# The extra block of a quantile graph network: 16-bit words from the collection, one tree for three quantiles, half candidates in three tiles

## The chip, the cores and the metric

The kernel runs on one core of one Trainium2 chip. The metric is device time in microseconds (us). PE is TensorE (matmuls; PEld its weight loads), DVE VectorE, ACT ScalarE, POOL GpSimd, SP SyncE, which here issues DMAs. SBUF is the on-chip memory that the engines work in, PSUM the banks that TensorE writes to.

## The reference, cut to what matters

There are 16 graphs ("batches") of N = 1024 nodes with C = 64 channels and a dense 0/1 adjacency. Four layers follow each other, each of the form x = x + layer(relu(layernorm(x))). Layer 0 thins out the neighbours of a node, sorts the values of those that remain in each channel, and takes three quantiles, each between two order statistics:

```python
vals = jnp.where(nd[..., None], x[:, None, :, :], jnp.inf)
s = jnp.sort(vals, axis=2)
nv = nd.sum(2)
for tau, w in zip((0.25, 0.5, 0.75), (0.25, 0.5, 0.25)):
    pos = tau * jnp.maximum(nv - 1, 0)
    lo, hi = floor(pos), ceil(pos)
    v_lo, v_hi = s[..., lo, :], s[..., hi, :]        # cut: take_along_axis
    agg = agg + w * (v_lo + (pos - lo) * (v_hi - v_lo))
out = x + agg
y = relu(out @ W1 + b1) @ W2 + b2
```

So six order statistics (three quantiles, lower and upper) are wanted for each of 16 x 1024 x 64 places. Layers 1 to 3 are a gated unit, a small network over summed neighbours, and an attention, all with dense products with the adjacency.

## The kernel before, in words

**How an order statistic is found.** The nodes of a batch are sorted once per channel (`sort_pair`, L760-855). The sorted list of a channel is cut into words of neighbouring ranks, 56 in all (NW; 28, NH, in each half). For a node, one fp8 matmul over the neighbours (`ndT` from `prepare`, L858-957) and the words' weights (`wt`, `weights`, L958-) gives for each word and channel a number that holds both a count and a part of the place (L1096). ACT adds the wanted rank (the bias) and writes 16-bit integers (L1104). Among these DVE looks for the last word that is not past the rank: it adds 2048 for the second statistic of the quantile (L1162), and takes a tree of unsigned maxima over the words (L1167). Small integer arithmetic on the result (`places`, L1010-) gives masks. PE transposes the 16-bit words, ACT takes their sign (L1149, L1151), and matmuls with a table of the sorted values (L1196) leave for each channel a row of candidates in PSUM, from which DVE picks one with masked copies (`pick`, L1060-1068; L1204 in select) and adds it with its factor to `agg` (`add_to`, L1069-1073).

**A window and the extra block.** In `select` each quantile looks only at a window of the words. A few nodes need more; they are flagged, and up to 64 of them in a batch (ROOM) are done once more over all 56 words. `compact` (up to L1302) runs at the end of each batch's `select`: it numbers the flagged nodes, writes the flags (L1237), gathers their neighbour rows, forms the words with the same weights (L1287, seven pieces of 512 numbers), copies each piece from PSUM to `xr` as 32-bit numbers (L1291), and SP stores one or two pieces to the DRAM buffer `x_d` (L1292). It also stores a selection matrix, transposed, to `sel_d`. The first batch of a pair has partitions 0 to 63, the second 64 to 127, so a pair's extra rows are one tile. `x_d` has one place, used again in each pair.

`extras` (L1304-1371), the block that is changed, then does both batches' extra rows at once:
- four DMAs on ACT's queue (L1307) load `x_d` into `comb_x`, 128 x 3584 32-bit numbers; DVE clears two tables (L1311), and SP loads the values into them, four DMAs each; `qx` (L1319) is the bias for three quantiles
- for each quantile k: ACT writes `y_x` (L1325), 16 transposes (L1332) go to a `tr` tile, two signs (L1335) are taken, DVE adds 2048 (L1339), takes a tree of maxima over 28 rows (L1003 and L1007 in `maxima`), and the last two operations give `z_x` and `odd_x` (L1345, L1346)
- `places` for all six statistics together
- for each of six statistics: 64 matmuls fill `cand` (L1356; one tile of four PSUM banks), five masked copies pick (L1064), one operation adds to `agg_x` (L1071, L1073)
- for each of the two batches: SP loads `sel_t` (L1364, one buffer), eight matmuls in fp32 put the rows back at their nodes (L1367; 16 records on PE), and a masked copy writes them into `aggs[i]` (L1368).

**The order of work.** A loop over 8 pairs (L1619-1654) calls `weights` and `select` for both batches, `extras`, and `layers` for both (L1466-1585; the first operation that needs `aggs` is L1471), and in the same scope `prepare` and `sort_pair` for the next pair. A scheduler lays out a fixed order on each engine at build time, by priorities and estimated times, so work of the next pairs is interleaved with `extras` and `layers`. Each engine runs its list in order; SP's and ACT's lists also hold the DMAs that they issue, and a DMA issue that waits holds up what is behind it. Tiles are reused as soon as their last reader is done, which the waits express. The neighbour tables of the layers are loaded by SP (L1452); the weights start with a load of `y_d` (L965), which the end of `sort_pair` (L847, L852, L853, L855) stores, an addition (L969) and the weights themselves (L974).

A general branch behind the loop does a batch again where there were more than 64 flagged nodes; it isn't entered with this input.

Of the kernel before, what the change touches and what calls it, by code (L numbers as in the profile page):

```python
# [9 lines left out]
F32 = mybir.dt.float32  # L10
BF16 = mybir.dt.bfloat16
# [12 lines left out]
P = 128  # L24
# [10 lines left out]
NW = 56  # L35
# [7 lines left out]
def gnn_stack(ctx, tc, x, adj, nodemask, w, out):  # L43
# [24 lines left out]
    nc.vector.tensor_scalar(offdiag, ident, -1.0, 1.0, op0=ALU.mult, op1=ALU.add)  # L68
    ones_b = const.tile([P, N], BF16, name="ones_b")
    nc.vector.memset(ones_b, 1.0)  # L70
# [90 lines left out]
    nc.vector.memset(ttab, 0.0)  # L161
    x_d = dram.tile([P, NW * C], F32, name="x_d")
    sel_d = dram.tile([2, P, NT, P], F32, name="sel_d")
# [291 lines left out]
    def general(gw):  # L455
# [47 lines left out]
        with tc.For_i(0, B, 1) as b:  # L503
            with ExitStack() as per_batch:
# [13 lines left out]
                with (  # L518
# [4 lines left out]
                    kept = nb1.tile([P, NT, N], BF16, name="kept")  # L523
                    notrem = nb1.tile([P, NT, N], BF16, name="notrem")
                    for t in range(NT):
                        a = nb2.tile([P, N], F32, name="a", bufs=3)
# [9 lines left out]
                        cum = nb2.tile([P, N], F32, name="cum")  # L536
                        nc.vector.tensor_tensor_scan(cum, ones_b, ni, 0.0, op0=ALU.mult, op1=ALU.add)

# [520 lines left out]
    def pick(cand, masks):  # L1059

        v = cand.rearrange("p q (d l) -> p q d l", l=24)
        for (dst, frm, n), mk in zip(PICKS, masks):
            mk = mk.rearrange("p (q d o) -> p q d o", d=4, o=1)
            nc.vector.copy_predicated(  # L1064
                v[:, :, :, dst : dst + n], mk.to_broadcast([P, NQ, 4, n]), v[:, :, :, frm : frm + n]
            )
        return v[:, :, :, 11]
# [158 lines left out]
    def compact(b, i, wt, row10, out_of, kept, cp, cpp):  # L1226
# [39 lines left out]
        nc.vector.tensor_copy(who, pv[:, 9:10])  # L1266
        nc.scalar.copy(vx[mine, :], pv[mine, :9])
        rows = cp.tile([P, N], F8, name="rows")
        nc.gpsimd.indirect_dma_start(
# [3 lines left out]
        for j0 in range(0, NT, 4):  # L1273
# [5 lines left out]
            nc.scalar.copy(ndx[:, j0 : j0 + 4, :], px, saturate=False)  # L1279
        for u in range(0, len(PIECES), 2):  # L1280
            two = PIECES[u : u + 2]
            n = len(two) * 512
            xr = cp.tile([P, 1024], F32, name="xr")
            for e, g in enumerate(two):
                pw = bank()
                for j in range(NT):
                    nc.tensor.matmul(  # L1287
                        pw, ndx[:, j, :], wt[g][:, j].rearrange("p w c -> p (w c)"),
                        start=(j == 0), stop=(j == NT - 1),
                    )  # L1290
                nc.scalar.copy(xr[mine, e * 512 : (e + 1) * 512], pw[mine])  # L1291
            nc.sync.dma_start(x_d[mine, two[0] * 512 : two[0] * 512 + n], xr[mine, :n])  # L1292
        sel_t = cp.tile([P, NT, P], F32, name="sel")
# [7 lines left out]
    def extras(pr, kept, aggs, xs, xp):  # L1301

        vx = kept["vx"]
        comb = xs.tile([P, NW * C], F32, name="comb_x")  # L1304
        for u in range(0, len(PIECES), 2):
            at = slice(PIECES[u] * 512, (PIECES[u] + len(PIECES[u : u + 2])) * 512)
            nc.scalar.dma_start(comb[:, at], x_d[:, at])  # L1307
        tabs = []
        for i in range(2):
            tab = xs.tile([4 * NH, NQ, 4, 48], F16, name=f"tab{i}")  # L1310
            nc.vector.memset(tab, 0.0)  # L1311
            for d in range(4):
                taken = nc.sync.dma_start(
                    tab[d : 4 * NH : 4, :, d, :],
                    t_d[(pr * 2 + i) * C : (pr * 2 + i + 1) * C, :NH].rearrange("(q d) h e -> d h q e", d=4)[d],
                )
            tabs.append(tab)
        qx = xs.tile([P, 3], F32, name="qx")
        nc.vector.tensor_scalar(qx, vx[:, :3], -2048.0, -2048.0, op0=ALU.mult, op1=ALU.add)  # L1319
        signs = []  # L1320
        z = xs.tile([P, 1, 6, C], U16, name="z_x")
        odd = xs.tile([P, 1, 6, C], U16, name="odd_x")
        for k in range(3):
            y = xs.tile([P, 2, 2 * NQ, 4 * NH], I16, name="y_x", bufs=2)
            nc.scalar.activation(  # L1325
                y[:, 0].rearrange("p r (h d) -> p r h d", d=4),
                comb.rearrange("p (h r d) -> p r h d", r=2 * NQ, d=4),
                AF.Identity, bias=qx[:, k : k + 1], scale=1.0,
            )
            pt = xp.tile([P, 2, 512], F32, name="tr").bitcast(BF16).rearrange("p e (q n) -> p (e q) n", n=P)  # L1330
            for q in range(NQ):
                nc.tensor.transpose(pt[: 4 * NH, q, :], y[:, 0, q, :].bitcast(BF16), ident_b)  # L1332
            for s in range(2):
# [4 lines left out]
                signs.append(sign)  # L1338
            nc.vector.tensor_scalar_add(y[:, 1], y[:, 0], 2048.0)  # L1339
            yu = y.bitcast(U16)  # L1340
            maxima(yu, NH)
            ev, od = yu[:, :, :NQ, :4], yu[:, :, NQ:, :4]
            zs = z[:, 0, 2 * k : 2 * k + 2, :].rearrange("p s (q d) -> p s q d", d=4)
            os_ = odd[:, 0, 2 * k : 2 * k + 2, :].rearrange("p s (q d) -> p s q d", d=4)
            nc.vector.tensor_tensor(zs, ev, od, op=ALU.max)  # L1345
            nc.vector.tensor_tensor(os_, od, ev, op=ALU.is_gt)  # L1346
        marks = places(xs, z, 6 * C, 1)
        aggx = xs.tile([P, C], F32, name="agg_x")
        ag = aggx.rearrange("p (q d) -> p q d", d=4)
        for s in range(6):  # L1350
            cand = xp.tile([P, NQ, P], F32, name="cand")
            for q in range(NQ):
                for part in range(2):
                    for i in range(2):
                        mine = slice(i * ROOM, (i + 1) * ROOM)
                        nc.tensor.matmul(  # L1356
                            cand[mine, q, :96], signs[s][:, q, mine], tabs[i][:, q, :, part * 24 : (part + 1) * 24],
                            start=(part == 0), stop=(part == 1),
                        )
            v = pick(cand[:, :, :96], [mk[:, 0, s, :] for mk in (odd, *marks)])  # L1360
            add_to(ag, s == 0, v, vx[:, 3 + s : 4 + s])
        for i in range(2):
            sel_t = xs.tile([P, NT, P], F32, name="sel_t")
            nc.sync.dma_start(sel_t, sel_d[i])  # L1364
            ps = xp.tile([P, 2, 512], F32, name="tr")[:, 0, :].rearrange("p (t c) -> p t c", c=C)
            for t in range(NT):
                nc.tensor.matmul(ps[:, t, :], sel_t[:, t, :], aggx, start=True, stop=True)  # L1367
            nc.vector.copy_predicated(  # L1368
                aggs[i], kept["flag"][i].rearrange("p (t o) -> p t o", o=1).to_broadcast([P, NT, C]), ps
            )  # L1370
# [331 lines left out]
```

## Time and profile before

| | |
|---|---|
| median of three runs | 5883.57 us (5877.19 to 5884.53) |
| the profiled execution | 5867.21 us |
| its span, first to last instruction | 5865.4 us |
| mean granted TensorE clock | 0.84 of full speed |
| ACT busy | 3801.4 us (65%) |
| PE busy | 4372.7 us (75%) |
| L1325, ACT, 128x3584 | 24 times, 3277 ns |
| L1291, ACT, 64x512 | 112 times, 580 ns; idle before them 134.6 us for the stores x_d |
| L1356, PE, 112x96 | 3072 matmuls, 109.3 us |
| L1064, DVE, 128x768 / 128x256 / 128x128 / 128x64 | 956 / 420 / 287 / 221 ns |
| L1367, PE, one batch | 3.65 us |

The page gives busy time of an engine as a share of the span, and digits for 40 slices, where 9 means 90% or more. A stretch's line gives the busy time of each engine in it. A line of the timeline gives the start, the length, engine, line of code, operation, output and inputs, shapes and number of instructions; in brackets stands how long the engine was idle before and what released it. Events that the text uses, in us from the start of the span:

| pair (0 to 7) | its first L1096 | second flags L1237 | first memset L1311 | end of the second L1368 |
|---|---|---|---|---|
| 3 | 2373.0 | 2748.7 | 2802.3 | 2909.8 |
| 4 | 3072.8 | 3448.1 | 3498.9 | 3609.1 |
| 5 | 3779.4 | 4154.7 | 4207.4 | 4316.3 |
| 7 (last) | 5193.8 | 5548.2 | 5591.1 | 5668.7 |

### The profile page before, as it was taken

How to read it: one execution, taken by the hardware profiler on the slowest of the kernel's cores; microseconds unless marked ns; L12 is line 12 of the kernel's file. 1: busy time of each engine (PE TensorE's matmuls, PEld its weight loads, DVE VectorE, ACT ScalarE, POOL GpSimd, SP SyncE). 2: the span in 40 equal slices, each digit the busy share in tenths (PEclk: the TensorE clock that was granted, in tenths of full speed). 3: DMA queues.
4: the chain of work that ended last, by engine and by line, in shares of the span. 5: the costliest groups of instructions: out<-in, count | busy, mean ns of one | idle time of the engine just before them, and what ended most of it. 6: DMA issues, size and time to landing. Idle time of an engine off the chain costs nothing.

```text
span 5865.4 us, 114417 instructions
## 1 busy us (share of the span) xinstructions
PE 4372.7 (75%) x45010; PEld 2736.6 (47%) x45010; DVE 5066.1 (86%) x13175; ACT 3801.4 (65%) x5752; POOL 180.9 (3%) x292
## 2 busy tenths in 40 slices
PE   1488677885868857788577876788677895878856
PEld 1355443554435544455434554355443554435532
DVE  9899888988899897998889988899888998877744
ACT  1587657676576855777567666677657775577724
POOL 3000000000000000000000000000000000000000
PEclk5699778997889968899689986899878997789967
DMA  4401273013631056210561125501264013620023
GB/s 127 125 27 41 89 221 116 27 31 124 207 98 36 20 156 217 63 40 29 172 203 45 37 77 168 172 35 34 89 206 132 27 32 120 208 81 19 11 88 127
DMA packets 524420, 568.23 MB, mean 97 GB/s; under 512 B 263808, under 2 KB 413568, under 8 KB 523872
## 3 DMA queue, kind: packets, MB, share of 16 engines
q1 hardware_dynamic: 381472, 476.43, 26.0%
q10 hardware_dynamic: 140064, 81.84, 4.6%
q8 instruction: 355, 5.82, 0.4%
q0 software_dynamic: 2336, 2.57, 0.2%
q14 instruction: 193, 1.58, 0.1%
HBM read 376.95 MB, written 183.76 MB: 96 GB/s over the span
## 4 chain that ended last, share of the span: by engine, by line
PE 27%; DVE 23%; ACT 14%; DMA 10%; issue 3%; SPq 0%; POOL 0%; ACTq 0%; DVEq 0%; POOLq 0%
PE comb L1096 7%; DVE y L1167 5%; PE cand L1196 4%; DMA adjT<-a_d 4%; PE bank L1459 4%; ACT sign L1151 3%; PE comb L1287 3%; DMA a_d<-at 2%; ACT y L1104 2%; DVE cand L1204 2%; DVE att L1570 2%; DVE adjT L1563 1%; DVE y L1162 1%; DVE cum L878 1%; DVE wt L974 1%
## 5 line engine op out<-in xcount | busy, mean ns | idle before, releaser
L1096 PE MATMUL comb<-wt,ndT 128*128 128x512 fp8e5 x6144 | 1422.3, 383 | 119.5 <-ACT sign L1151 98.1
L1104 ACT ACTIVATE y<-comb,qb 128x512 int16<-128x512 f32 x1152 | 742.5, 711 | 479.4 <-PE comb L1096 479.0
L1096 PEld LDWEIGHTS <-ndT 128*128 128x128 fp8e5 x6144 | 587.6, 98 | 837.4 <-issue 196.9
L1196 PE MATMUL cand<-vtab,sign 128*128 128x48 f16 (+1 forms) x18432 | 678.8, 192 | 60.9 <-DVE agg L1071 32.4
L1196 PEld LDWEIGHTS <-sign 128*128 128x128 fp8e5 x18432 | 651.5, 97 | 118.6 <-issue 57.2
L1151 ACT ACTIVATE sign<-comb,lower 128x1024 fp8e5<-128x1024 int16 (+1 forms) x640 | 693.2, 1083 | 0.0
L1151 ACT ACTIVATE sign<-comb,half 128x1024 fp8e5<-128x1024 int16 (+1 forms) x640 | 688.0, 1075 | 0.0
L1167 DVE TENSOR_TENSOR y<-y 128x512 uint16<-128x512 uint16 (+5 forms) x896 | 668.7, 788 | 16.6 <-PE comb L1149 16.2
L1204 DVE COPY_PREDICATED cand<-w_f,cand 128x256 f32<-128x256 uint16 (+1 forms) x1536 | 533.7, 376 | 95.8 <-PE cand L1196 92.6
L886 ACT COPY at<-pk 128x512 f32<-128x512 f32 x256 | 147.4, 586 | 394.5 <-PE pk L884 219.0
L1149 PE MATMUL comb<-ident_b,y 128*128 128x128 bf16 x4608 | 318.1, 222 | 93.5 <-ACT sign L1151 59.6
L1459 PE MATMUL bank<-adjT,nd 128*64 128x512 f32 x1024 | 314.1, 668 | 77.6 <-DMA adjT<-a_d 75.7
L1149 PEld LDWEIGHTS <-y 128*128 128x128 bf16 x4608 | 294.6, 99 | 118.9 <-issue 117.9
L928 PE MATMUL pk<-minus_b,rem 128*128 128x128 bf16 x1024 | 225.3, 246 | 158.2 <-ACT rem L909 158.2
L1459 PE MATMUL bank<-att,hs 128*64 128x512 f32 x512 | 199.9, 863 | 155.0 <-ACT hs L1575 154.9
L928 PE MATMUL pk<-ident_b,ni 128*128 128x128 bf16 x1024 | 220.5, 243 | 122.0 <-ACT ndT L934 65.0
L878 DVE TENSOR_TENSOR_SCAN cum<-ni 128x1024 f16<-128x1024 fp8e5 x128 | 291.8, 2283 | 11.0 <-POOL ni L874 10.9
L884 PE MATMUL pk<-ident,a 128*128 128x128 f32 x1024 | 189.5, 336 | 136.8 <-DMA a<-in_adj_dram 102.5
L974 DVE TENSOR_SCALAR wt<-node 128x2048 uint8<-128x2048 f16 x224 | 268.8, 1216 | 13.9 <-PE comb L1287 13.7
L774 DVE TENSOR_TENSOR s<-s 128x512 f32<-128x512 f32 (+1 forms) x440 | 275.6, 626 | 0.0
L1162 DVE TENSOR_SCALAR y<-y 128x4608 int16<-128x4608 int16 x128 | 173.4, 1355 | 118.0 <-ACT y L1104 117.7
L775 DVE TENSOR_TENSOR s<-s 128x512 f32<-128x512 f32 (+1 forms) x440 | 274.4, 624 | 0.0
(373 smaller groups left out, 8301.5 us busy)
## 6 DMA issues: line engine op xcount, KB each, us to landing
adjT<-a_d SPq DMA_DIRECT2D x384, 512.0 KB
a<-in_adj_dram SPq DMA_DIRECT2D x128, 512.0 KB
a_d<-at ACTq DMA_DIRECT2D x256, 256.0 KB
m_d<-swapped SPq DMA_DIRECT2D x104, 512.0 KB
swapped<-m_d SPq DMA_DIRECT2D x104, 512.0 KB
n_d<-nat SPq DMA_DIRECT2D x128, 128.0 KB
x_d<-xr SPq DMA_DIRECT2D x48, 256.0 KB
comb_x<-x_d ACTq DMA_DIRECT2D x24, 512.0 KB
```

Of the source, the lines that this page charges most:

```text
L774: nc.vector.tensor_tensor(to_lo, lo, hi, op=ALU.max)
L878: nc.vector.tensor_tensor_scan(cum[:, t - t0, :], ni[:, t, :], wide[:, t, pad - 1 : pad - 1 + N], 0.0, op0=ALU.add, op1=ALU.add)
L928: nc.tensor.matmul(pk[:, n % 4, :], lhs, rhs, start=(n % 4 == 0 and m == 0), stop=(m == len(terms) - 1 and last),)
L974: nc.vector.tensor_scalar(wt[g][:, :, k : k + 4, :].bitcast(U8), node, 4.0 * (25 + CODE * (8 * g + k)), 4.0 * 26, op0=ALU.add, op1=ALU.min,)
L1096: nc.tensor.matmul(pw, ndT[:, j, t * P : (t + 1) * P], wt[1 + g8][:, j].rearrange("p w c -> p (w c)"), start=(j == 0), stop=(j == NT - 1),)
L1104: nc.scalar.activation(y[:, 0, chunks, at : at + 8 * d_].rearrange("p q (w d) -> p q w d", d=d_), pw.rearrange("p (w q d) -> p q w d", w=8 ...
L1149: nc.tensor.transpose(pt[:, q - q0, :], y[:, 0, q, :].bitcast(BF16), ident_b)
L1151: nc.scalar.activation(signs[tl][s][:, q0:q1, :], pt.bitcast(I16), AF.Sign, bias=before[s], scale=-1.0, saturate=False,)
L1167: nc.vector.tensor_tensor(v[:, :, :, :n], v[:, :, :, :n], v[:, :, :, n : 2 * n], op=ALU.max)
L1196: nc.tensor.matmul(cand[:, e, at : at + 12 * d_].rearrange("p (d l) -> p d l", l=12), signs[tl][sec][:, chunk, :], tab[:, q, :, half_ * 12 ...
L1204: nc.vector.copy_predicated(v[:, :, :, dst : dst + k], mk.to_broadcast([P, 2, C // 2, k]), v[:, :, :, frm : frm + k])
L1459: nc.tensor.matmul(po[to : to + C, :], lhs, rhs[:, f * HALF : (f + 1) * HALF], start=(j == 0), stop=(j == NT - 1))
```

## The change

- `compact` writes 16-bit integers at once: for each piece three ACT operations, one for each quantile, with the bias `qx` (now made there by DVE), in an order of elements in which a chunk's 32 words lie together. `xr` has two buffers, and each piece is stored by itself (7 stores a batch, 14 a pair; now 8).
- `x_d` holds [128, 7 pieces, 3 quantiles, 512] 16-bit numbers. `extras` loads them with 12 DMAs on ACT's queue straight into `y_x`, for all three quantiles. L1325 and `comb_x` are gone.
- POOL clears the tables instead of DVE.
- The 48 transposes read strided words out of `y_x`; all of them, and the candidates and the last products, use three tiles of two PSUM banks (`two`).
- One addition of 2048 for all three quantiles, one tree for all six statistics; z and odd come from four operations.
- Candidates are made and picked in halves of 8 chunks, so 12 halves with 32 matmuls, five masked copies and one accumulation each.
- Both `sel_t` are loaded by two DMAs on ACT's queue into the place of `y_x`, ahead of the candidates.
- A constant row of ones is shortened from 1024 to 128 columns; the general branch makes its own.

```diff
-    x_d = dram.tile([P, NW * C], F32, name="x_d")
+    x_d = dram.tile([P, 7, 3, 512], I16, name="x_d")
...
         nc.scalar.copy(vx[mine, :], pv[mine, :9])
+        qx = cp.tile([P, 3], F32, name="qx")
+        nc.vector.tensor_scalar(qx[mine], pv[mine, :3], -2048.0, -2048.0, op0=ALU.mult, op1=ALU.add)
...
-            xr = cp.tile([P, 1024], F32, name="xr")
...
-                nc.scalar.copy(xr[mine, e * 512 : (e + 1) * 512], pw[mine])
-            nc.sync.dma_start(x_d[mine, two[0] * 512 : two[0] * 512 + n], xr[mine, :n])
+        for g in PIECES:
+            xr = cp.tile([P, 3, 512], I16, name="xr", bufs=2)
...
+            for k in range(3):
+                nc.scalar.activation(
+                    xr[mine, k].rearrange("p (h d r) -> p h r d", h=4, d=4),
+                    pw[mine].rearrange("p (h r d) -> p h r d", r=2 * NQ, d=4),
+                    AF.Identity, bias=qx[mine, k : k + 1], scale=1.0,
+                )
+            nc.sync.dma_start(x_d[mine, g], xr[mine])
...
-        comb = xs.tile([P, NW * C], F32, name="comb_x")
-        for u in range(0, len(PIECES), 2):
-            at = slice(PIECES[u] * 512, (PIECES[u] + len(PIECES[u : u + 2])) * 512)
-            nc.scalar.dma_start(comb[:, at], x_d[:, at])
+        y = xs.tile([P, 2, 3, 7, 512], I16, name="y_x")
+        for g in (1, 3, 5, 0):
+            for k in range(3):
+                here = slice(g, g + (2 if g else 1))
+                nc.scalar.dma_start(y[:, 0, k, here], x_d[:, here, k])
...
-            nc.vector.memset(tab, 0.0)
+            nc.gpsimd.memset(tab, 0.0)
...
-            y = xs.tile([P, 2, 2 * NQ, 4 * NH], I16, name="y_x", bufs=2)
-            nc.scalar.activation(
-                y[:, 0].rearrange("p r (h d) -> p r h d", d=4),
-                comb.rearrange("p (h r d) -> p r h d", r=2 * NQ, d=4),
-                AF.Identity, bias=qx[:, k : k + 1], scale=1.0,
-            )
-            pt = xp.tile([P, 2, 512], F32, name="tr").bitcast(BF16).rearrange("p e (q n) -> p (e q) n", n=P)
+            pt = xp.tile([P, 1024], F32, name="two", bufs=3).bitcast(BF16).rearrange("p (q n) -> p q n", n=P)
+            by_word = y[:, 0, k].rearrange("p g (w r) -> p r (g w)", w=16)
             for q in range(NQ):
-                nc.tensor.transpose(pt[: 4 * NH, q, :], y[:, 0, q, :].bitcast(BF16), ident_b)
+                nc.tensor.transpose(pt[: 4 * NH, q, :], by_word[:, q].bitcast(BF16), ident_b)
...
-            nc.vector.tensor_scalar_add(y[:, 1], y[:, 0], 2048.0)
-            yu = y.bitcast(U16)
-            maxima(yu, NH)
+        nc.vector.tensor_scalar_add(y[:, 1], y[:, 0], 2048.0)
+        yu = y.bitcast(U16).rearrange("p s k g n -> p (s k) g n")
+        for n, m in ((3, 4), (2, 2), (1, 1)):
+            nc.vector.tensor_tensor(yu[:, :, :n], yu[:, :, :n], yu[:, :, m : m + n], op=ALU.max)
+        yw = yu[:, :, 0]
+        for n in (256, 128):
+            nc.vector.tensor_tensor(yw[..., :n], yw[..., :n], yw[..., n : 2 * n], op=ALU.max)
...
         marks = places(xs, z, 6 * C, 1)
+        sel_t = xs.tile([P, 2, 3, 7, 512], I16, name="y_x").rearrange("p s k g n -> p (s k g n)")
+        sel_t = sel_t[:, : 4 * NT * P].bitcast(F32).rearrange("p (i t n) -> p i t n", i=2, n=P)
+        for i in range(2):
+            nc.scalar.dma_start(sel_t[:, i], sel_d[i])
         aggx = xs.tile([P, C], F32, name="agg_x")
...
-            cand = xp.tile([P, NQ, P], F32, name="cand")
-            for q in range(NQ):
+            for q0 in range(0, NQ, 8):
+                cand = xp.tile([P, 1024], F32, name="two", bufs=3).rearrange("p (q n) -> p q n", n=P)
+                for q in range(8):
...
-            v = pick(cand[:, :, :96], [mk[:, 0, s, :] for mk in (odd, *marks)])
-            add_to(ag, s == 0, v, vx[:, 3 + s : 4 + s])
+                here = slice(q0 * 4, (q0 + 8) * 4)
+                v = pick(cand[:, :, :96], [mk[:, 0, s, here] for mk in (odd, *marks)])
+                add_to(aggx[:, here].rearrange("p (q d) -> p q d", d=4), s == 0, v, vx[:, 3 + s : 4 + s])
         for i in range(2):
-            sel_t = xs.tile([P, NT, P], F32, name="sel_t")
-            nc.sync.dma_start(sel_t, sel_d[i])
-            ps = xp.tile([P, 2, 512], F32, name="tr")[:, 0, :].rearrange("p (t c) -> p t c", c=C)
+            ps = xp.tile([P, 1024], F32, name="two", bufs=3)[:, : NT * C].rearrange("p (t c) -> p t c", c=C)
             for t in range(NT):
-                nc.tensor.matmul(ps[:, t, :], sel_t[:, t, :], aggx, start=True, stop=True)
+                nc.tensor.matmul(ps[:, t, :], sel_t[:, i, t, :], aggx, start=True, stop=True)
```

## The prediction

> **What bounds the kernel now.** I read the page first (engine shares, the 40 slices), then a table of 20 us stretches over one middle pair of batches, then the groups by shape, and last the timeline of the last pair around the extra block.
>
> ```profile
> span 5865.4 us, 114417 instructions
> ...
> PE 4372.7 (75%) x45010; PEld 2736.6 (47%) x45010; DVE 5066.1 (86%) x13175; ACT 3801.4 (65%) x5752; POOL 180.9 (3%) x292
> DVE  9899888988899897998889988899888998877744
> ```
>
> DVE carries 86% of the span; only the last three slices fall off: those are the layers of the last pair, where nothing is left to lie beside them. So there are two regimes. In pairs 0 to 6 a pair takes about 705 us (first L1096 of pair 4 at 3072.8 us, of pair 5 at 3779.4), of which DVE idles some 77. There the price of an edit is mostly its DVE work, and what it moves counts only if DVE stalls. After the last pair's extra block comes a chain of latencies up to the end of the program. Stretches from pair 3's extra block into pair 4's select (columns: length, busy PE, PEld, DVE, ACT, POOL, clock, DMA share, GB/s):
>
> ```profile
> 2800.00:2820.00 20.00, 2.29 (x18) 1.87 (x17) 14.87 (x30) 8.54 (x5) 1.76 (x4) 0.56 0.60 179
> 2840.00:2860.00 20.00, 11.79 (x133) 9.35 (x133) 19.83 (x54) 14.12 (x27) 0.53 (x1) 0.66 0.34 111
> 3020.00:3040.00 20.00, 15.19 (x155) 8.02 (x154) 12.87 (x42) 15.06 (x20) 0.00 (x0) 1.00 0.79 253
> 3220.00:3240.00 20.00, 16.54 (x176) 10.03 (x172) 20.00 (x55) 19.27 (x31) 0.00 (x0) 1.00 0.10 36
> ```
>
> The extra block lies in the first two. DVE loses 5 us in the first and nothing in the second, since sorting and neighbour work of later pairs is interleaved there. DVE loses more at 3020 to 3040 (the end of the layers and the way into the next weights) than in the extra block. In select it is full. The last pair has nothing to interleave (start, us, engine, line, form, idle before and its releaser):
>
> ```profile
> 5594.13 6.46 ACT L1325 ACTIVATE y_x<-comb_x,qx 128x3584 int16<-128x3584 f32 x2 [12.74 <-DVE qx L1319]
> ...
> 5628.29 2.77 PE L1356 MATMUL cand<-tab,sign_x 112*64 112x96 f16 x64 [13.82 <-DVE agg_x L1071]
> 5631.10 0.96 DVE L1064 COPY_PREDICATED cand<-odd_x,cand 128x768 f32<-128x768 uint16 x1 [2.87 <-PE cand L1356]
> ...
> 5664.30 3.65 PE L1367 MATMUL tr<-agg_x,sel_t 128*128 128x64 f32 x16 [3.83 <-DMA sel_t<-sel_d]
> 5667.99 0.72 DVE L1368 COPY_PREDICATED agg<-flag,tr 128x512 f32<-128x512 uint16 x1 [6.76 <-PE tr L1367]
> 5668.61 0.68 DVE L1471 TENSOR_TENSOR nd<-nd,agg 128x512 f32<-128x512 f32 x1
> ```
>
> The reader sees PE and DVE taking turns over one `cand` tile (2.87 us waiting in each turn, five turns), and the second `sel_t` load waiting for its buffer. All of it is ahead of the first layers' operation, with no cover.
>
> **Last pair, step by step.** DVE leaves select at 5590.9 in both versions.
> (1) The collection. Now each piece needs an ACT copy of 0.58 us (L1291, 64x512) and waits for its store (3.05 us at 5576.8, with one buffer). Afterwards there are three 16-bit copies a piece: nearest row L1291's 0.58, above it the permuted L1104 with 0.71. That is 28 copies more a pair, 16 to 24 us of ACT, against waits for stores of 134.6/8 = 16.8 us a pair that the second buffer takes away, and 3 x 3.28 = 9.8 us of L1325 that goes. I take ACT as even. The gather grows from 4 issues to 12, and from 1.83 to 2.75 MB; 4 issues now take 3.28 us in pair 3, so 8 more cost up to 6.6, most of them before the last store. The data landed at 5588.8; I take 5591, with 5588.8 and 5595.4 as ends.
> (2) L1325 in front of DVE and PE goes: DVE now begins L1339 at 5597.44, afterwards at about 5591.
> (3) Add and tree: rows 3584 in 1.09 us; maxima of 3584 in 2.02 and 1792 in 1.085, so 0.15 us plus 0.52 ns an element. Now 3 x (1.09 + 4.5) = 16.8 us. Afterwards one add (2.9 to 3.3) and maxima of 9216, 6144, 3072, 1536, 768: 11.6. With four z/odd operations (1 us) z is ready at about 5607; now 5619.6.
> (4) `places` with the first picks took 5619.7 to 5627.7, so 8 us: 5615. Signs do not come later: 48 transposes (16 in 1.96 us) end at 5597, six signs of 1.96 end at about 5605. They read strided words, which no row shows; were transposes twice as slow, signs would end near 5607, still ahead. POOL's clearing of `tab` (nearest: its 128x2048 memset, 1.80 us) should be done by 5596 (an estimate from that row, twice, with 1.5 for the larger tile), and the tables landed before the first mask.
> (5) Candidates: half a tile is 32 matmuls of 43 ns, 1.39 us on PE. Three tiles let PE run ahead by three halves. A half's picks cost 0.152 us plus elements/0.96 GHz for 384, 128, 128, 64 and 32, and an accumulate: 1.77 us when each waits for the former. The new DVE order weaves two halves; where select does that now, two picks take 2.98 us. I take 1.45 for PE and DVE together. Some two of twelve halves lie in `places`, ten follow: last accumulate at 5629.5 (now 5656.7).
> (6) Both `sel_t` loads go ahead on ACT's queue into the place of y_x. Two groups of 3.65 follow directly, then L1368: layers begin at about 5638, now 5668.6.
> The sum is **30 us less**. With the late landing and 1.8 us a half: 22; with picks at 1.2 and the early landing: 35. Layers behind it wait for this operation, and SP, no longer holding a `sel_t` load back, issues their first loads sooner; I see no cause for them to give it back, but their table loads (L1452) could land no earlier: then up to 8 us return.
>
> **Pairs 0 to 6.** DVE work per pair: two memsets of 1.338 go (-2.7), add -0.3, tree -1.9, picks +2.3 (36 operations more, 0.065 us each as woven) to +6.7 (at 1.77). Net -2.6 to +1.8, so about zero.
> What matters is the order (numbers of pair 3 into pair 4). I charged the DVE order of both built programs, from the end of select, with rows' durations. From the second flags (L1237) to the add it is 49.6 now, 50.7 then. From there to the last L1368 it shrinks from 86.7 to 50.2 us: the cover (24 us of sorting, 10 of neighbours) moves behind the block. The block would then end some 36 us sooner, at 2874 instead of 2909.8. It must now run on its own pace, about the 47 us of the last pair; DVE work of 50 still covers it.
> The layers are a chain of 201 us (2909.8 to about 3111). Started 36 us earlier, it ends near 3075. But the first weights operation L974 now has 40 us of layers work before it and 35 behind; then all 75 lie before it. DVE work up to L974 grows from 259 to 293 us: at 2748.7 + 293 and the stalls of now (48 us less the 6 to 8 that the block gives up) 3083 to 3089, now 3056. From L974 to the next flags it falls from 368 to 333; with the 24 us of stalls that lie there now, the next flags come at 3440 to 3446, now 3448.
> One new stall: the last sorting operation leads over L847, L852, L853 (1.05 + 0.66 + 0.59 at least) to the store L855, the load `node` L965 and then L969. Now 23.6 us of DVE work cover this, then 4.7. In pair 3 it takes from L811 at 3022.7 to past 3041, with PE full; if alone, from these durations and two transfers, 9 to 11. So 4 to 6 us of stall, 14 at worst (flags then at 3444 to 3460), and PE, whose weights come later, idles some 13 us that select does not ask for while DVE is full.
> The bounds per pair: -8 (the stalls in the block go, nothing new) to +10 (the chain exposed, the picks at 1.77). I take **-2** (3446), between the sums without and with the new stall, so -14 over seven pairs.
>
> **Rules against it.** The rows say 0.152 us fixed for a pick and 0.065 where woven. The Trainium skill, "VectorE: DVE Perf Modes", section "The TRN2 errata", says that each instruction pays its latency again and that small tiles should be avoided; from its measured 150 cycles I estimate 36 x 0.156 = 5.6 us a pair, 3 more than by the woven row, in all 26 us less gain. The clearing of `tab` leaves DVE for POOL (1.80 us nearby). "SBUF — State Buffer", section "SBUF: two separate sides", says that a GpSimd instruction and a DVE instruction in a two-port mode block each other entirely; by it some of the 2.7 us would come back as waiting. No row of before has the two side by side.
>
> **Rivals.**
> (a) Forecast: tail -30, pairs -2 each: 5867.2 - 30 - 14 = 5823. Chance 0.48.
> (b) The block's stalls in the middle pairs are won too (11 us of idle DVE there now), -8 each with the same tail: 5867.2 - 30 - 56 = 5781. For: the turns of 2.87 us vanish there as well. Against: the second stretch above has DVE at 19.83 of 20. Chance 0.20.
> (c) Nothing: the woven picks or the ACT copies (28 x 0.71 = 20 us, in select where ACT has 19.27 of 20) cost 4 a pair: 5867.2 - 30 + 28 = 5865. Chance 0.15.
> (d) Slower: the chain from sorting to L969 stands open in each pair, and the layers' own gaps, no longer beside weights, add to it: 10 a pair, 5867.2 - 30 + 70 = 5907. It decides from 30/7 = 4.3 us a pair. For: DVE at 12.87 of 20 in that place already; against: PE and ACT work of the next pair starts early enough to feed select. Chance 0.17.
>
> **Numbers.** The profiled execution took 5867.2 us (span 5865.4); the median of the three runs is 5883.6, 16.4 more, which I add: (a) 5840, (b) 5798, (c) 5881, (d) 5924. The likeliest, 5840, has its own range of 5812 to 5868 (per pair -6 to +2). The range for 8 in 10 takes in (b) with some of its spread and (c), and half of (d): 5786 to 5912. Within 0.2% (11.8 us, about what a measurement can tell) is (c); faster (a) and (b), 0.68; slower (d), 0.17.
>
> **What would show it.** In the last pair: first layers' operation (L1471 of before) at about 5638; z by 5607; candidate halves 1.4 to 1.5 apart; no wait for `sel_t`. In middle pairs: last L1368 about 36 us earlier, L974 about 30 later, next flags within 8 of now, and a DVE wait for `node` of 4 to 6 us. I am wrong if y lands after 5596, if halves come 1.8 or more apart, or if that wait is over 10 us.

## The result, and the profile after

The changed kernel is slower: 6329.03 us in the median of four runs (6307.92 to 6335.03) against 5883.25 us, a ratio of 1.0753 (95% interval 1.0727 to 1.0780). The forecast was 5840 us, a gain. The profiled execution took 6327.28 us.

The page of the changed kernel, the lines that answer to those of before (the last two give the busy share of DVE and ACT in 40 slices):

```profile
span 6325.4 us, 115008 instructions
...
PE 4544.1 (72%) x45010; PEld 2805.8 (44%) x45010; DVE 5087.1 (80%) x13319; ACT 4410.8 (70%) x5952; POOL 236.7 (4%) x308
...
DVE  9997689886897968977789777897778976886744
ACT  2578757786678756787577784678757787578844
```

DVE does the same work (5087 us, 5066 before) in a span that is 460 us longer, so it waits. ACT does 609 us more. The groups by shape say which: first the changed kernel's copies out of PSUM, the transposes that wait for them, and the masked copies of select (columns: busy us, mean ns of one, idle before and its releaser),

```profile
L1293 ACT ACTIVATE xr<-comb,qx 64x512 int16<-64x512 f32 x336 | 757.8, 2694 | 46.1 <-PE comb L1288 45.9
...
L1206 DVE COPY_PREDICATED cand<-w_f,cand 128x256 f32<-128x256 uint16 x1024 | 416.9, 424 | 527.6 <-PE cand L1198 525.7
...
L1303 PE MATMUL comb<-ident,sel 128*128 128x128 f32 x128 | 35.7, 434 | 139.8 <-ACT xr L1293 139.8
```

then the copies and the masked copies of before:

```profile
L1204 DVE COPY_PREDICATED cand<-w_f,cand 128x256 f32<-128x256 uint16 x1024 | 418.4, 421 | 94.8 <-PE cand L1196 92.6
...
L1291 ACT COPY xr<-comb 64x512 f32<-64x512 f32 x112 | 61.8, 580 | 201.5 <-DMA x_d<-xr 134.6 <-PE comb L1287 66.9
```

One copy takes 2694 ns, not 580 to 711. The records of neighbours overlap a little, so the 336 of them keep ACT busy for 757.8 us (2.26 each), where 112 took 61.8. How that reaches DVE is seen in stretches over a `compact` and the extra block of pair 3 of the changed kernel (columns as above: length, PE, PEld, DVE, ACT, POOL, clock, DMA share, GB/s):

```profile
2980.00:3000.00 20.00, 8.06 (x23) 3.19 (x22) 0.71 (x2) 20.00 (x10) 0.00 (x0) 0.75 0.18 44
3000.00:3020.00 20.00, 10.10 (x158) 9.57 (x158) 11.49 (x27) 19.45 (x12) 1.39 (x2) 0.67 0.29 89
3060.00:3080.00 20.00, 6.03 (x63) 4.47 (x63) 20.00 (x54) 15.00 (x27) 0.00 (x0) 0.50 0.24 79
3315.00:3335.00 20.00, 8.99 (x116) 6.01 (x112) 11.69 (x60) 7.23 (x12) 0.00 (x0) 0.67 0.36 73
```

In the first, ACT is busy all 20 us with ten instructions and DVE does 0.71 us. In the third, the extra block itself, DVE is full: the block is not where the time goes. The fourth is the way into the next weights, where DVE idles 8 of the 20 us. The timeline of the last pair's `compact` shows the links of the chain:

```profile
6018.27 40.37 ACT L1293 ACTIVATE xr<-comb,qx 64x512 int16<-64x512 f32 x18 [2.85 <-PE comb L1288]
...
6038.66 3.35 PE L1288 MATMUL comb<-wt,ndx 128*128 128x512 fp8e5 x8 [3.39 <-ACT xr L1293]
6045.32 1.12 PE L1303 MATMUL comb<-ident,sel 128*128 128x128 f32 x4 [3.31 <-ACT xr L1293]
...
6051.98 1.12 PE L1303 MATMUL comb<-ident,sel 128*128 128x128 f32 x4 [5.42 <-ACT xr L1293]
6052.89 3.40 PE L1198 MATMUL cand<-vtab,sign 128*128 128x48 f16 x69
6055.52 1.55 DVE L1206 COPY_PREDICATED cand<-w_f,cand 128x256 f32<-128x256 uint16 x4 [27.96 <-PE cand L1198]
```

18 copies stand on ACT for 40 us. PE's next piece needs a PSUM tile that ACT has not emptied, the transposes of the selection matrix (L1303) too, and in PE's fixed order the last candidates of select (L1198) are behind those. DVE waits 27.96 us for them. Over the whole execution DVE waits 525.7 us for L1198, where it waited 92.6 us for the same matmuls (L1196) before.

From the second flags of pair 0 to those of pair 7 a pair takes 762.7 us, 702.5 before: 60.2 more, seven times, is 421 of the 460 us. Pair 0 up to its second flags gives 30, the stretch from the last pair's flags to the end 8.

### The profile page after: what moved, and what is told of

It reads as the page before. It is cut to its first block, busy times and chain, and to the rows that moved or that the text cites. A ratio compares the mean times of both kernels' runs of the same rounds, so it can differ in the third digit from the quotient of the medians.

```text
span 6325.4 us, 115008 instructions
## 1 busy us (share of the span) xinstructions
PE 4544.1 (72%) x45010; PEld 2805.8 (44%) x45010; DVE 5087.1 (80%) x13319; ACT 4410.8 (70%) x5952; POOL 236.7 (4%) x308
## 3 DMA queue, kind: packets, MB, share of 16 engines
q0 software_dynamic: 2336, 2.57, 0.2%
## 4 chain that ended last, share of the span: by engine, by line
PE 32%; DVE 27%; ACT 24%; DMA 11%; issue 5%; POOL 0%; SPq 0%; ACTq 0%; DVEq 0%; POOLq 0%
PE comb L1098 12%; ACT xr L1293 9%; ACT sign L1153 6%; DMA adjT<-a_d 5%; PE cand L1198 5%; DVE y L1169 4%; PE bank L1469 4%; ACT y L1106 2%; DVE cand L1206 2%; DMA a<-in_adj_dram 2%; PE pk L930 2%; DVE wt L976 1%; DVE cum L880 1%; DVE att L1580 1%; DVE y_x L1340 1%
## 5 line engine op out<-in xcount | busy, mean ns | idle before, releaser
L1098 PE MATMUL comb<-wt,ndT 128*128 128x512 fp8e5 x6144 | 1483.6, 395 | 158.6 <-ACT sign L1153 111.8
L1098 PEld LDWEIGHTS <-ndT 128*128 128x128 fp8e5 x6144 | 601.5, 100 | 904.8 <-issue 300.9
L1206 DVE COPY_PREDICATED cand<-w_f,cand 128x256 f32<-128x256 uint16 (+1 forms) x1536 | 531.9, 379 | 528.2 <-PE cand L1198 525.7
L1293 ACT ACTIVATE xr<-comb,qx 64x512 int16<-64x512 f32 x336 | 757.8, 2694 | 46.1 <-PE comb L1288 45.9
L1198 PE MATMUL cand<-vtab,sign 128*128 128x48 f16 (+1 forms) x18432 | 692.3, 194 | 29.9 <-DVE agg L1075 22.9
L1198 PEld LDWEIGHTS <-sign 128*128 128x128 fp8e5 x18432 | 668.5, 98 | 92.0 <-issue 22.3
L1288 PE MATMUL comb<-wt,ndx 128*128 128x512 fp8e5 x896 | 272.5, 471 | 164.3 <-ACT xr L1293 160.3
L930 PE MATMUL pk<-ident_b,ni 128*128 128x128 bf16 x1024 | 233.4, 249 | 193.5 <-ACT at L888 113.2
L936 ACT ACTIVATE ndT<-pk 128x512 fp8e5<-128x512 f32 (+3 forms) x352 | 158.1, 477 | 214.7 <-PE pk L930 178.6
L776 DVE TENSOR_TENSOR s<-s 128x512 f32<-128x512 f32 (+1 forms) x440 | 277.3, 630 | 0.0
```

What stands on the lines that cost most here:

```text
L776: nc.vector.tensor_tensor(to_lo, lo, hi, op=ALU.max)
L930: nc.tensor.matmul(pk[:, n % 4, :], lhs, rhs, start=(n % 4 == 0 and m == 0), stop=(m == len(terms) - 1 and last),)
L1098: nc.tensor.matmul(pw, ndT[:, j, t * P : (t + 1) * P], wt[1 + g8][:, j].rearrange("p w c -> p (w c)"), start=(j == 0), stop=(j == NT - 1),)
L1198: nc.tensor.matmul(cand[:, e, at : at + 12 * d_].rearrange("p (d l) -> p d l", l=12), signs[tl][sec][:, chunk, :], tab[:, q, :, half_ * 12 ...
L1206: nc.vector.copy_predicated(v[:, :, :, dst : dst + k], mk.to_broadcast([P, 2, C // 2, k]), v[:, :, :, frm : frm + k])
L1293: nc.scalar.activation(xr[mine, k].rearrange("p (h d r) -> p h r d", h=4, d=4), pw[mine].rearrange("p (h r d) -> p h r d", r=2 * NQ, d=4), ...
```

## The experiments

Theory A: the copies write 16-bit numbers one by one at a step of 32 numbers (64 bytes), which makes them slow, and they are the whole loss; what else was reckoned holds. Rival B: the new static order of the instructions is the loss. Rival C: any permuted 16-bit copy out of PSUM on 64 partitions is slow.

**read_strided**

```diff
-                    xr[mine, k].rearrange("p (h d r) -> p h r d", h=4, d=4),
-                    pw[mine].rearrange("p (h r d) -> p h r d", r=2 * NQ, d=4),
+                    xr[mine, k].rearrange("p (h d r) -> p h d r", h=4, d=4),
+                    pw[mine].rearrange("p (h r d) -> p h d r", r=2 * NQ, d=4),
```

> The changed kernel, with one thing undone: the three ACT copies of a piece (L1293) walk the elements in the order of the destination, so that they write 16-bit numbers side by side and read PSUM with a step of four 32-bit numbers; the layout in memory and all that follows is the same. Theory A (the write step of 64 bytes makes the copy slow, 2694 ns where 580 to 711 was reckoned, and the copies are the loss): 0.6 to 0.75 us a copy, and the time comes to 5815 to 5870 us, since the rest was reckoned rightly. Rival B (the new static order is the loss: weights of the next pair begin 224 us after the extra block's end, 147 before, and the copies lie beside other work): the copies get shorter, the time stays above 6200. Rival C (any permuted 16-bit copy out of PSUM on 64 partitions is slow): copies of 2 us or more, time above 6200.

Measured: 5838.89 us, 0.9908 of before (0.9895 to 0.9922), 490 us under the changed kernel. The copies in its groups by shape:

```profile
L1293 ACT ACTIVATE xr<-comb,qx 64x512 int16<-64x512 f32 x336 | 201.5, 675 | 93.8 <-PE comb L1288 46.9 <-DMA x_d<-xr 46.6
```

The same numbers at the same places, walked in another order, in 675 ns. Theory A holds. B falls: PE, DVE, ACT and POOL run the same instructions in the same order as in the changed kernel (their lists in the two traces agree line for line), and the next weights begin 223 us after the end of pair 3's block, 224 in the changed kernel and 147 before. C falls: the copy is permuted still, on the read side.

**one_of_three**: the first quantile's copies keep the step, the other two write side by side.

```diff
-            for k in range(3):
+            nc.scalar.activation(
+                xr[mine, 0].rearrange("p (h d r) -> p h r d", h=4, d=4),
+                pw[mine].rearrange("p (h r d) -> p h r d", r=2 * NQ, d=4),
+                AF.Identity, bias=qx[mine, 0:1], scale=1.0,
+            )
+            for k in range(1, 3):
                 nc.scalar.activation(
-                    xr[mine, k].rearrange("p (h d r) -> p h r d", h=4, d=4),
-                    pw[mine].rearrange("p (h r d) -> p h r d", r=2 * NQ, d=4),
+                    xr[mine, k].rearrange("p (h d r) -> p h d r", h=4, d=4),
+                    pw[mine].rearrange("p (h r d) -> p h d r", r=2 * NQ, d=4),
```

> As read_strided, but the copy for the first quantile keeps the order of the changed kernel, so a third of the copies writes with the step of 64 bytes. Theory A with a proportional price: those copies 2.7 us, the others 0.6 to 0.75; time a third of the way from read_strided to the changed kernel, near 6000. If the second buffer and the work beside it hide a part: less than a third, 5840 to 5900. Rival B: above 6200 as in every kernel with this order.

Measured: 5996.27 us, one run. That is 157 of 490 us, 0.32 of the way, so the loss is about in proportion to the number of slow copies. There are 112 of them at 2502 ns, and 224 at 801, a little over the 0.6 to 0.75 us expected.

**step_sweep**: each piece n writes, or reads, with another step S (2, 4, 8, 16, 32, 64, 128).

```diff
+            def by(v, S):
+                return v.rearrange("p (b s) -> p s b", s=S)
+            def flat(v, S):
+                return v.rearrange("p (s b) -> p s b", s=S)
+            if n == 0:
+                nc.scalar.activation(by(xr[mine, 0], 2), flat(src, 2), AF.Identity, bias=b0, scale=1.0)
+                nc.scalar.activation(flat(xr[mine, 1], 2), by(src, 2), AF.Identity, bias=b1, scale=1.0)
...
```

> The copies of the seven pieces write (first quantile) or read (second quantile) with steps of 2, 4, 8, 16, 32, 64, 128 elements, one line of code each; the third is plain for five pieces, writes runs of four numbers for the sixth, and is as in the changed kernel for the seventh. The words come out in the wrong order, so the output is not the reference's; only the lengths of the copies are read. Theory A: plain and all reads 0.57 to 0.75 us; writes grow with the step and reach 2.7 us at 32 elements, with a break at a step that the row shows. Rival C: all copies with a step are near 2.7 us, reads too.

Groups by shape. L1324 writes without a step, L1326 in runs of four, L1303, L1306, L1309 and L1315 with steps of 2, 4, 8 and 32 numbers; L1307 and L1316 read with steps of 4 and 32:

```profile
L1324 ACT ACTIVATE xr<-comb,qx 64x512 int16<-64x512 f32 x80 | 54.0, 674 | 0.0
...
L1309 ACT ACTIVATE xr<-comb,qx 64x512 int16<-64x512 f32 x16 | 40.7, 2545 | 7.1 <-DMA x_d<-xr 7.1
...
L1315 ACT ACTIVATE xr<-comb,qx 64x512 int16<-64x512 f32 x16 | 39.9, 2497 | 0.0
...
L1306 ACT ACTIVATE xr<-comb,qx 64x512 int16<-64x512 f32 x16 | 22.2, 1388 | 0.0
...
L1316 ACT ACTIVATE xr<-comb,qx 64x512 int16<-64x512 f32 x16 | 14.8, 923 | 0.0
...
L1303 ACT ACTIVATE xr<-comb,qx 64x512 int16<-64x512 f32 x16 | 13.3, 829 | 47.7 <-PE comb L1288 47.7
L1326 ACT ACTIVATE xr<-comb,qx 64x512 int16<-64x512 f32 x16 | 11.0, 690 | 0.0
L1307 ACT ACTIVATE xr<-comb,qx 64x512 int16<-64x512 f32 x16 | 10.9, 681 | 0.0
```

The price grows from 4 to 16 bytes of step (829, 1388, 2545 ns) and stays there (2451 to 2566 up to a step of 256 bytes; 2497 at 32 numbers, where 2.7 us was expected). Reading PSUM with any step costs 0.65 to 0.94 us, from 32 bytes on more than the 0.75 expected. Runs of four cost almost nothing (690). L1104, the row that the forecast took as the upper neighbour, reads in runs of at least four numbers but writes in runs of at least 32, and shows 0.71.

**who_pays_for_steps**: single copies of other kinds.

```diff
+            wide = cp.tile([P, 512], F32, name="wide")
...
+                nc.scalar.activation(by(wide[mine], 32), flat(src, 32), AF.Identity, bias=b0, scale=1.0)
...
+                nc.scalar.activation(by(xr[mine, 2], 32), flat(wide[mine], 32), AF.Identity, bias=b2, scale=1.0)
...
+                nc.vector.tensor_scalar(by(xr[mine, 2], 32), flat(src, 32), b2, None, op0=ALU.add)
...
```

> Single copies, one line of code each, to tell what the price of the step hangs on: ACT with a 32-bit destination and steps of 2, 4 and 32 elements (8, 16 and 128 bytes), ACT from SBUF in place of PSUM, ACT with pairs of 16-bit numbers at a step of 32, ACT on 128 partitions in place of 64, and DVE with 16-bit destinations at a step of 32, from PSUM and SBUF, beside the same without a step. The words come out wrong and one buffer holds xr, so only the lengths of the copies are read. If the price is ACT's alone and hangs on the step in bytes from 16 on: 32-bit at 16 and 128 bytes 2.4 to 2.6 us, pairs 1.2 to 1.4, DVE with a step as without (0.6 to 0.7). If it is SBUF's write side for any engine: DVE with a step 2 us or more too. If it hangs on numbers under 32 bits: 32-bit copies 0.6 to 0.75 at every step.

In it, `by(v, S)` and `flat` are those of step_sweep. ACT, from SBUF at a step of 32 (L1313), 32-bit destination at steps of 16, 128 and 8 bytes (L1306, L1309, L1315), pairs of 16-bit numbers at a step of 32 (L1316); then DVE, from SBUF and PSUM at a step of 32 (L1325, L1307), and without a step from PSUM and SBUF (L1310, L1328):

```profile
L1313 ACT ACTIVATE xr<-wide,qx 64x512 int16<-64x512 f32 x16 | 40.8, 2549 | 0.5
...
L1306 ACT ACTIVATE wide<-comb,qx 64x512 f32<-64x512 f32 x16 | 18.5, 1157 | 0.0
L1309 ACT ACTIVATE wide<-comb,qx 64x512 f32<-64x512 f32 x16 | 18.1, 1129 | 0.0
L1315 ACT ACTIVATE wide<-comb,qx 64x512 f32<-64x512 f32 x16 | 11.2, 702 | 0.0
L1316 ACT ACTIVATE xr<-comb,qx 64x512 int16<-64x512 f32 x16 | 10.8, 674 | 0.0
...
L1325 DVE TENSOR_SCALAR xr<-wide,qx 64x512 int16<-64x512 f32 x16 | 57.8, 3614 | 0.3
L1307 DVE TENSOR_SCALAR xr<-comb,qx 64x512 int16<-64x512 f32 x16 | 39.1, 2444 | 47.6 <-ACT wide L1306 47.6
L1310 DVE TENSOR_SCALAR xr<-comb,qx 64x512 int16<-64x512 f32 x16 | 12.0, 748 | 2.7 <-ACT wide L1309 2.5
...
L1328 DVE TENSOR_SCALAR xr<-wide,qx 64x512 int16<-64x512 f32 x16 | 7.7, 478 | 0.3
```

The second of the three expectations is met, the first and the third are not. The price is not ACT's alone: DVE pays 2444 instead of 748 ns, and from SBUF 3614 instead of 478. The copy's time is high for single 16-bit numbers, about a half of that (1.13 to 1.16 us) for 32-bit numbers at 16 bytes or more, and that of a plain copy for pairs of 16-bit numbers. Why pairs go free at the same step is open. On 128 partitions only a plain 32-bit copy was run (589 ns, 673 on 64), so the price of a step there is not shown.

**collection_only**: the kernel before with the new collection (in read_strided's manner) alone; one tree for each quantile, one candidate tile of four banks, tables by DVE, `sel_t` by SP.

```diff
-            y = xs.tile([P, 2, 2 * NQ, 4 * NH], I16, name="y_x", bufs=2)
-            nc.scalar.activation(
...
+            y = y3[:, k]
+            by_word = y[:, 0].rearrange("p g (w r) -> p r (g w)", w=16)
...
```

> The kernel before with the new collection alone, in read_strided's manner (16-bit words, three copies a piece that write side by side, 12 loads straight into y_x, no L1325); the tree stays one for each quantile (over the new layout), one tile of four banks for the candidates, tables cleared by DVE, sel_t by SP. It separates the collection from the rest. If the collection is even, as the forecast had it for ACT, and the tail gains only what L1325 cost there (3.3 us ahead of DVE, 12 us with the three turns): 0.994 to 1.002 of before. If the collection carries read_strided's gain: 0.990 to 0.993. If one tile for the candidates is the hindrance that one_cand_tile showed, with the cover moved away: slower than before, 1.005 to 1.03.

Measured: 5882.29 us, 0.9989 (0.9977 to 1.0002): no difference, as the first case had it. The collection by itself gives nothing even with fast copies; the 0.9% of read_strided come only with the rest, which this run does not split.

**one_cand_tile**

```diff
-            pt = xp.tile([P, 1024], F32, name="two", bufs=3).bitcast(BF16).rearrange(...)
+            pt = xp.tile([P, 1024], F32, name="two", bufs=2).bitcast(BF16).rearrange(...)
...
-                cand = xp.tile([P, 1024], F32, name="two", bufs=3).rearrange(...)
+                cand = xp.tile([P, 1024], F32, name="cand").rearrange(...)
...
```

The transposes and the last products so have two tiles instead of three, beside the one for the candidates.

> read_strided with the half candidates in one tile of two banks instead of three. Theory A (the turns of PE and DVE are what the tail saves): halves come 2.4 to 3.0 us apart in the last pair instead of 1.23, so the last L1378 is 14 to 20 us later; in the other pairs the block has no cover left either, so 0 to 15 us a pair more, and the time is 20 to 100 us above read_strided. Rival: PE fills the one tile while DVE works on other things; time within 10 us of read_strided.

Measured: 6046.26 us, 1.0274 (1.0242 to 1.0306), 207 us above read_strided: the expectation's first case, the turns of PE and DVE, and worse than its range. Its last pair:

```profile
5807.05 1.49 PE L1366 MATMUL cand<-tab,sign_x 112*64 112x96 f16 x32 [2.10 <-DVE agg_x L1073]
5808.58 0.56 DVE L1066 COPY_PREDICATED cand<-odd_x,cand 128x384 f32<-128x384 uint16 x1 [1.59 <-PE cand L1366]
...
5810.33 0.25 DVE L1075 SCALAR_TENSOR_TENSOR agg_x<-cand,vx,agg_x 128x32 f32<-128x32 f32 x1
5810.64 1.49 PE L1366 MATMUL cand<-tab,sign_x 112*64 112x96 f16 x32 [2.10 <-DVE agg_x L1075]
```

PE and DVE take turns; halves are 3.6 us apart. In read_strided they come 1.2 and 1.4 us apart in turn, 1.3 on the mean. From the addition to the last masked copy pair 3 takes 112 us, against 63.5. From flags to flags a pair takes 25.7 us more (at most 15 were expected), and the last pair's block 27 us more (14 to 20 were expected).

**sel_by_sp**

```diff
-        for i in range(2):
-            nc.scalar.dma_start(sel_t[:, i], sel_d[i])
...
+            sel_t = xs.tile([P, NT, P], F32, name="sel_t")
+            nc.sync.dma_start(sel_t, sel_d[i])
```

> read_strided with the selection matrices loaded as before the change: SP's queue, one buffer, at the place of use. If the forecast's step 6 is right, the second matrix comes 3.8 us late again in every pair and the last, with the loads of the layers behind it: 3 to 5 us in the tail, 0 to 4 us in each other pair, so 3 to 30 us above read_strided. Rival: hidden, within 3 us.

Measured: 5829.37 us, 0.9915 (0.9885 to 0.9944): the same as read_strided. From the addition to the last masked copy it is 58.0 instead of 52.6 us in the last pair, and 4 to 5 more in pair 3, but the layers take the latter back. This is the rival's case: step 6 is true in its place and too small to be seen in the time.

**tree_in_two**

```diff
-        for n, m in ((3, 4), (2, 2), (1, 1)):
-            nc.vector.tensor_tensor(yu[:, :, :n], ...)
+        for part in (slice(3, 6), slice(0, 3)):
+            yp = yu[:, part]
+            for n, m in ((3, 4), (2, 2), (1, 1)):
+                nc.vector.tensor_tensor(yp[:, :, :n], ...)
...
```

> read_strided with the tree of maxima in two passes, the second statistic of each quantile (the half that the addition writes) first. In read_strided's last pair the one tree waits 5.39 us after the addition, until the last of the 48 transposes has read the half that it overwrites. If that wait is what the tail lacks against the forecast (z at 5614.8, forecast 5607): z comes some 5 us sooner after the addition in the last pair, five operations more cost 0.75 us a pair, and the time is 0 to 5 us under read_strided. If the signs and candidates are what z waits beside: the last L1378 moves by less than 2 us.

Measured: 5800.56 us, 0.9849 (0.9813 to 0.9885): faster than read_strided, and than before by 1.5%. The wait for the transposes falls from 40.5 to 18.8 us in eight pairs. Pair 3 takes 59.3 us from the addition to the last copy instead of 63.5. In the last pair that stretch shrinks by 2.3 us, not 5; over the seven pairs the gain builds up to 31 us, which the expectation had not seen: the wait lies open in every pair. The 22 us less of this wait are the larger part of the gain; the rest is not split.

**four_loads**: tree_in_two with four loads of the words instead of 12.

```diff
-    x_d = dram.tile([P, 7, 3, 512], I16, name="x_d")
+    x_d = dram.tile([P, 3, 7, 512], I16, name="x_d")
...
-            nc.sync.dma_start(x_d[mine, g], xr[mine])
+            nc.sync.dma_start(x_d[mine, :, g], xr[mine])
...
-            for k in range(3):
-                here = slice(g, g + (2 if g else 1))
-                nc.scalar.dma_start(y[:, 0, k, here], x_d[:, here, k])
+            here = slice(g, g + (2 if g else 1))
+            nc.scalar.dma_start(y[:, 0, :, here], x_d[:, :, here])
```

> tree_in_two with the 12 loads of the words as 4 (all three quantiles in one DMA; x_d is laid out by quantile, so that the packets are twice as long). In read_strided's last pair the last nine issues stand on ACT's queue for 10.2 us and the data come 12.3 us after the last copy; forecast were 7.6. If issues and packets set that: 3 to 6 us sooner in the tail, up to 4 us of ACT in each other pair, 5 to 30 us under tree_in_two. Rival: the stores and the way through DRAM set it: within 8 us of tree_in_two.

Measured: 5800.95 us, 0.9856 (0.9834 to 0.9877): the same as tree_in_two, the rival's case. DVE's waits ahead of the addition fall from 27.2 to 8.8 us in eight pairs, those ahead of the tree rise from 19.1 to 29.9: the transposes are what comes next.

**sort_first**: tree_in_two with `sort_pair` called ahead of the layers.

```diff
+                    if pr + 1 < pairs:
+                        sort_pair(pr + 1, cur, sop)
                     for i, (ly, lb) in enumerate(((ly0, lb0), (ly1, lb1))):
...
-                        sort_pair(pr + 1, cur, sop)
```

> tree_in_two with the sorting of the next pair called ahead of the layers, not behind them. In read_strided DVE does 11.6 us of work in the 20 us before the first weights, with waits of 2.0, 3.0 and 3.2 us, which the way from the last sorting operation over the store of y_d to the weights sets. If that is a loss, the weights begin 5 to 10 us sooner after the block and the time falls by 30 to 60 us. Rival: DVE's total work sets the pair, or the sorting delays the layers' chain by as much: within 15 us of tree_in_two, or above it.

Measured: 6165.83 us, 1.0491 (1.0457 to 1.0524): 365 us worse than tree_in_two, the rival's case. From the block's end to the next weights it takes 290 us in pair 3 instead of 219, with 49.5 us of idle DVE instead of 30.6. Delaying the layers' chain costs more than the short stall ahead of the weights. The expectation also misread that stall: in pair 3 of read_strided its waits are for PE (2.0 us, L947) and for loads of `x` (3.0 and 3.2 us, L695), not for `y_d`.

The quickest version found is tree_in_two, with four_loads beside it.

## Why the prediction was wrong, by its own steps

- **Step 1, the collection: this is the step that failed.** It charged 28 more copies a pair at 0.58 to 0.71 us and called ACT even. The changed copy differed from both rows in the order in which it wrote, and neither row writes single 16-bit numbers at a step. Such an operation should have had its cost bounded from both sides; instead two rows of the same size stood for it. It took 2.69 us: a pair's 42 copies keep ACT busy for 94.7 us (757.8/8), in read_strided for 25.2 (201.5/8). Of these 69.5 us more, 61 reach the pair's time (762.7 us from flags to flags, 701.4 in read_strided).
- **Rival (c) named the ACT copies, at 0.71 us, and rival (d) the slower side, by the weights' chain.** Neither was the mechanism, and the 8-in-10 range ended 400 us too low.
- **The rest held in its order, as read_strided shows, but that its sum is met to 1 us is luck.** Forecast 5840, measured 5839; pair 3's block to end at 2874, measured 2874.0; the weights some 30 us later than before, measured 36 to 46 in pairs 1 to 6; a pair 2 us shorter, measured 1.1 ((4909.6 - 4917.2)/7). The terms were less good. A gain of 44 us (30 and 14) was forecast; the span of the profiled execution is 24 us shorter than before, and the median is 52 us under that of the runs of before beside it (5873 to 5896). In pair 3 DVE idles 20.8 us up to the block's end (21.1 before; 6 to 8 less were forecast), then 37.8 up to the weights (23.6 before), then 13.3 up to the next flags (26.8 before, taken as unchanged). The wait for `node` of 4 to 6 us is in no middle pair; only ahead of the last pair's weights does it come, with 8.2 us.
- **The tail was forecast too short.** Forecast: layers begin 30 us sooner; measured 20.7 (5647.9). z came at 5614.8, not 5607: the addition began at 5592.9 (forecast 5591), and the tree waited 5.39 us for the transposes whose source it overwrites; these took 9.35 us where 5.9 were reckoned. Halves came faster than 1.45 us, at 1.3. In the end the first layers' operation waited 2.4 us for its own load, which was issued only when the last selection matmul was done.
- **Picks.** The lengths of the rows, added up, give 5.7 us a pair (21.2 against 15.5); the prediction's 6.7, from the same rows, should have been that. But records overlap where operations are woven. Counted each only up to the start of the next operation, picks and accumulations take 15.5 us a pair in read_strided and 12.8 before: 2.7 more, near the 2.3 of the woven row. The Trainium skill, "VectorE: DVE Perf Modes", section "The TRN2 errata", gave an estimate of 5.6 by its fixed price per instruction, twice what these two traces show.
- **z and odd** were charged 1 us for four operations. They write single 16-bit numbers at a step of four numbers: 0.60 and 0.63 us for 192 elements, where 128 side by side took 0.22. That fits the price of a step, but no run has the same 192 elements side by side.
- **POOL's clearing** takes 2660 ns a table, and it holds DVE up. In the last pair of read_strided (DVE and POOL, other engines left out):

```profile
5555.93 6.00 DVE L1023 TENSOR_SCALAR w_m<-z 128x512 uint16<-128x512 uint16 x1
5556.50 5.28 POOL L1318 MEMSET tab<- 112x3072 f16 x2
...
5561.85 0.27 DVE L1023 TENSOR_SCALAR w_r<-z 128x512 uint16<-128x512 uint16 x1
```

The first takes 6.00 us, where the next of the same shape takes 0.27, and ends with the second clearing. In each of pairs 0 to 6 one L875 beside the second clearing takes 2.92 us, where the median is 0.69. In the kernel before and in collection_only, where DVE clears the tables, the operation of L875 never takes over 1.2 us. The Trainium skill, "SBUF — State Buffer", section "SBUF: two separate sides", says that a GpSimd instruction and a DVE instruction in a two-port mode block each other; these rows agree with it, with the 6.00 and 2.92 us. So 2.2 of the 2.7 us that the forecast took off each pair came back, and in the last pair up to 5.7 us.

- **The cover.** That DVE work of 50 us covers the block was right only with three tiles: with one, pair 3's block takes 112 us (one_cand_tile).

## What to carry to other kernels

When a change moves an operation to another order of elements, look at the innermost step of what it writes before taking a price from a row of the same size: if no row writes that way, put a copy of it alone on the chip, since one line in the other order was worth 490 us here. The permutation out of PSUM was cheap here on the read side (675 ns) and dear on the write side (2694). An operation that overwrites what another engine still reads waits for that reader, so start with the half that nobody reads (22 us less waiting in tree_in_two).

## What the runs showed of the hardware that was not expected

- Writing single 16-bit numbers to SBUF costs, for 64x512 on ACT, 0.67 us side by side, 0.83 at a step of 4 bytes, 1.39 at 8, and 2.45 to 2.57 from 16 to 256 bytes; on DVE at 64 bytes 2.44 from PSUM (0.75 side by side) and 3.61 from SBUF (0.48).
- For the same size, ACT writes 32-bit numbers in 0.67 us side by side, 0.70 at a step of 8 bytes, 1.16 at 16 and 1.13 at 128; runs of two or four 16-bit numbers take 0.67 to 0.69.
- Reading PSUM at a step costs ACT 0.65 to 0.68 us up to 16 bytes and 0.91 to 0.94 from 32 to 512.
- Weight loads on PE from words at a step of 64 bytes (the transposes of `extras`) took 283 ns on the mean, 210 from contiguous ones. In the last pair the granted clock was 0.50 beside both, and they took 283 and 212.
- While POOL cleared a table, some DVE operations ended only with the clearing (6.00 us for one of 0.27 to 0.29), and others ran beside it at their usual length (a scan of 2.28 us and masked copies of 0.22 and 0.29 in pair 3 of read_strided).
